# Graph layers on one core: neighbour rows by one-hot matmul for 60 buckets, by GpSimd row gathers for the other 38

## The chip, the cores and the metric

The kernel runs on one core of one Trainium2 chip. The metric is device microseconds of one execution. The kernel before was run 10 times; its median is the time that a change is measured against.

## The reference

A graph has N = 12500 nodes with 128 features and E = 200000 edges, sorted by `dst`. One gated layer is followed by three GIN layers; both parts end in a residual sum and a layernorm.

```python
# layer 0 (gnn)
msg      = (h[src] @ W_msg.T + b_msg) + edge_embed[edge_type]
messages = segment_sum(msg, dst)                  # rows of src are read, sums go to dst
x        = layernorm(x + gru_cell(messages, h))

# layers 1 to 3 (gin); every node also has an edge to itself
ee  = edge_attr @ enc_w + enc_b
h   = concat(x[dst], ee)          # layer 1: x[dst] + ee
agg = segment_sum(h, src)         # rows of dst are read, sums go to src
x   = relu(bn(agg @ w1 + b1)) @ w2 + b2
```

The last result is added to the layer's input `x` and normalised again.

## The kernel before

**Buckets and slots.** The nodes are cut into NB = 98 buckets of 128. Every pair (bucket summed into, bucket read from) is a cell with SL = 32 slots; a cell holds 20.8 edges on average. The few edges over 32 (some 190) go into an overflow list, which `spill(i)` adds by itself before each layer, 128 edges a round. The setup sorts the edges on chip under two keys (A and B), lists the overflow (`Listed`), and writes for each output bucket a row `inrow` (which row each slot reads) and columns `outcol` (which node each slot is summed into).

**One layer.** `layer(i, slot0)` goes over the output buckets o = 0 to 97. All feature rows of the graph, as three bfloat16 parts side by side (H3 = 384 columns, 768 bytes), lie in SBUF in 14 tiles `x0` to `x13` of 7 buckets each, loaded once a layer. For a bucket:

- `one_hots(o + 1)` loads the row `inrow` of the next bucket, broadcast to 128 partitions (`inr`, 784 KB, an SP transfer), and makes on DVE the gather matrix `g` in one compare (L1066) and the scatter matrix `s` in four (L1069).
- The 98 cells make 25 tiles of 128 slots, NTL = 25, in GROUPS = 9 groups of TG = 3 tiles. A group's gather is 12 matmuls (L1116) of 128 x 32, four of them beside each other in the array's column groups, from `x` into three PSUM banks `g` (two buffers). The result is evicted to `e` in bfloat16: in even groups two tiles on ACT (L1122) and one on DVE (L1123), in odd ones all three on ACT (L1125).
- One group later three scatter matmuls (L1087) multiply `e` by the scatter matrix and accumulate in the PSUM tile `acc` (one buffer). In layers 1 to 3 the bucket's own rows go into `acc` by one matmul with the identity (L1137); this is the edge of a node to itself.
- `finish(o)` adds the three parts in `acc` to the overflow sums (three adds on DVE, L1096 to L1098). After each odd bucket, the dense part of two buckets (`gru` in layer 0, `gin` after) is queued, and `tick()` emits a piece of it per group.

**Edge attributes.** The sums of `edge_attr` by `src` are the same for the three GIN layers and are made once by a generator, `attr`, in five steps per bucket. A step of `attributes()` issues 18 indirect DMAs on GpSimd back to back (L597; each brings 128 rows of 98 bytes), the others (`add_up`) make a one-hot on DVE, run 18 matmuls (L616), and store the result with an SP transfer. `gin` needs the sums of its buckets. The generator is stepped during the sort, and in layers 0 and 1 at these groups:

```python
                if slot0 is not None:
                    if k in (1, 5) or (k == 3 and o % 2):
                        next(attr, None)
```

That is 2.5 steps, half an attribute bucket, per output bucket.

**Order.** In the layers a scheduler orders each engine's instructions from the program and its tile dependencies. SP's queue carries `inr`, the overflow sums and the results; GpSimd's queue carries, within the layers, the attribute gathers alone, and between layers the spill's gathers (L501, L528, L554) and its write-back.

Of the kernel before, what the change touches and what calls it, by code (L numbers as in the profile page):

```python
# [18 lines left out]
H = 128  # L19
# [14 lines left out]

EP = 125
# [14 lines left out]
LCAP = E + 64  # L50
GL = 14
assert EP * EC == E and NB % GL == 0
# [3 lines left out]
def gnn_kernel(ctx: ExitStack, tc: tile.TileContext, x, xT, src, dst, ea, et, w_msg, w_ihT, w_hhT, b_msg,  # L56
# [256 lines left out]
    def xtiles(name):  # L313
        return [xpool.tile([P, XC, H3], BF16, name=f"x{k}") for k in range(NB // XC)]
# [4 lines left out]
    outcol = [cols.tile([P, NB, TC], BF16, name=f"outcol{i}") for i in range(2)]  # L319
# [4 lines left out]
    count = {k: ctile([1, 2], f"count{k}", I32) for k in "AB"}  # L324
# [9 lines left out]
    total = kp.tile([NB, 1], F32, name="total")  # L334
    startB = kp.tile([NB, 1], I32, name="startB")
# [140 lines left out]
    def starts():  # L476

        V.tensor_copy(cnt, cps[:NB, :NB])
        incl = kp.tile([NB, NB], F32, name="incl")
        V.tensor_tensor_scan(incl, ones[:NB, :NB], cnt, 0.0, op0=OP.mult, op1=OP.add)  # L480
        V.tensor_copy(total, incl[:, NB - 1:NB])
        rps = psa.tile([P, 512], F32, name="acc")
        T.matmul(rps[:NB, 0:1], before[:NB, :NB], total, start=True, stop=True)
        rst = kp.tile([NB, 1], F32, name="rst")
        V.tensor_scalar(rst, rps[:NB, 0:1], float(FRONT), None, op0=OP.add)
        V.tensor_copy(startB, rst)
        V.tensor_sub(incl, incl, cnt)
        V.tensor_scalar(start, incl, rst, None, op0=OP.add)


    def added(k, width, sources, target, pool_name):


        groups = nc.values_load(count[k][:, 1:2], min_val=0, max_val=LCAP // P,
                                skip_runtime_bounds_check_because="it counts groups of the edges")
        with tc.tile_pool(name=pool_name, bufs=1, side="right") as lp:
            with tc.For_i(0, groups, 1) as g:
                pos = lp.tile([P, 1], I32, name="pos")
                nc.sync.dma_start(pos, lists[k][bass.ds(g * P, P), :])
                key = lp.tile([P, 1], F32, name="key")  # L500
# [17 lines left out]
                node, rows = sources(top, field, lp)  # L518
# [27 lines left out]
    def spill(i):  # L546
        def sources(top, field, lp):
            s = lp.tile([P, 1], I32, name="s")
            V.tensor_add(s, top, field(11, 127))
            d = lp.tile([P, 1], I32, name="dd")  # L550
            V.scalar_tensor_tensor(d, field(18, 127), float(P), field(4, 127), op0=OP.mult, op1=OP.add)
            to, frm = (d, s) if i == 0 else (s, d)
            x3 = lp.tile([P, H3], BF16, name="x3")
            G.indirect_dma_start(out=x3, out_offset=None, in_=tables[i],  # L554
                                 in_offset=bass.IndirectOffsetOnAxis(ap=frm, axis=0))
            rows = lp.tile([P, H + NTX], F32, name="rows")
            V.tensor_tensor(rows[:, :H], x3[:, 0:H], x3[:, H:2 * H], op=OP.add)
            V.tensor_tensor(rows[:, :H], rows[:, :H], x3[:, 2 * H:], op=OP.add)
            if i:
                return to, rows[:, :H]  # L560
            t = lp.tile([P, 1], F32, name="t")
            V.tensor_copy(t, field(0, 15))
            V.tensor_scalar(rows[:, H:], iota[:, :NTX], t, None, op0=OP.is_equal)
            return to, rows

        added("A", H + NTX if i == 0 else H, sources, ovf[i], f"spill{i}")

    def spill_attributes():
        def sources(top, field, lp):
            s = lp.tile([P, 1], I32, name="s")  # L570
            V.tensor_add(s, top, field(18, 127))
            e3 = lp.tile([P, EW], BF16, name="e3")
            G.indirect_dma_start(out=e3, out_offset=None, in_=ea3,
                                 in_offset=bass.IndirectOffsetOnAxis(ap=field(0, (1 << 18) - 1), axis=0))
            rows = lp.tile([P, EA], F32, name="rows")
            V.tensor_copy(rows, e3[:, 0:EA])
            V.tensor_tensor(rows[:, 1:], rows[:, 1:], e3[:, EA:EA + DE], op=OP.add)
            V.tensor_tensor(rows[:, 1:], rows[:, 1:], e3[:, EA + DE:], op=OP.add)
            return s, rows

        added("B", EA, sources, ovfe, "spille")
# [100 lines left out]
    class Listed:  # L682
# [3 lines left out]
        def __init__(self, k, shift, bits):  # L686
            self.k, self.shift, self.bits = k, shift, bits
            self.stack = ExitStack()
            self.lp = self.stack.enter_context(tc.tile_pool(name=f"listed{k}", bufs=1, side="right"))
            t = lambda name, n, d=F32: self.lp.tile([P, n], d, name=name)  # L690
            self.back, self.same, self.at = t("back", SC), t("same", SC, I32), t("at", SC)
            self.first, self.base = t("first", 1), t("base", 1)
            self.m8, self.ok, self.row, self.spare, self.step = (t(n, 8) for n in ("m8", "ok", "row", "spare", "step"))
            self.rowi, self.val = t("rowi", 8, I32), t("val", 8, I32)
            self.num, self.most = t("num", 1), self.lp.tile([1, 2], F32, name="most")

        def mark(self, ahead):
# [18 lines left out]
            T.transpose(ps[0:1, 128:256], self.num, ident)  # L716
            G.iota(self.spare, pattern=[[P, 8]], base=LCAP, channel_multiplier=1,
# [11 lines left out]
            V.tensor_scalar(c[:, 1:2], self.most[:, 1:2], float(P - 1), None, op0=OP.add)  # L729
            V.tensor_single_scalar(c[:, 0:1], c[:, 0:1], 3, op=OP.logical_shift_right)  # L730
            V.tensor_single_scalar(c[:, 1:2], c[:, 1:2], 7, op=OP.logical_shift_right)
# [5 lines left out]
        def round(self):  # L737
# [7 lines left out]
            V.tensor_scalar(self.val, self.m8, self.base, None, op0=OP.add)  # L745
            for j in range(8):
# [5 lines left out]
        def rest(self):  # L752
            rounds = nc.values_load(count[self.k][:, 0:1], min_val=0, max_val=SC // 8,
                                    skip_runtime_bounds_check_because="it counts columns of the sort by eight")
            with tc.For_i(0, rounds, 1):
                self.round()

# [11 lines left out]
    def slots(cells):  # L769

        with tc.tile_pool(name="slots", bufs=1, side="right") as lp:
# [10 lines left out]
            def turned(rows, to):  # L782

                for t0 in range(0, NTL, 8):
                    n = min(8, NTL - t0)
# [32 lines left out]
            turned(sl, outcol[1])  # L818
# [5 lines left out]
            turned(ty, typecol)  # L824
            yield
# [32 lines left out]
    X = xtiles("0")  # L858
# [33 lines left out]
    with by_hand():  # L892
        la = Listed("A", SL, 18)
        for b in range(NB):
            runs(cells[:, b * SL:(b + 1) * SL], "A", start[:, b:b + 1], SL)
        for _ in la.mark(2):
            pass
# [155 lines left out]
    def layer(i, slot0):  # L1053
        a = 0 if i == 0 else 1
        wid = H3 + (NTX if i == 0 else 0)
        work = []

        def one_hots(o):

            inr = rp.tile([P, CW], BF16, name="inr")  # L1060
            nc.sync.dma_start(inr, inrow[a][o:o + 1, :].to_broadcast([P, CW]))
            g = ohp.tile([P, CW], BF16, name="g")
            st = ohp.tile([P, P, TC], BF16, name="s")
            ready.append((g, st))
            yield
            V.tensor_scalar(g, inr, pidx, None, op0=OP.is_equal)  # L1066
            yield
            for f0 in range(0, P, P // 4):
                V.tensor_tensor(st[:, f0:f0 + P // 4, :], iotas[:, f0:f0 + P // 4, :],  # L1069
                                outcol[a][:, o, None, :].to_broadcast([P, P // 4, TC]), op=OP.is_equal)  # L1070
                yield

# [4 lines left out]
        ready = []  # L1077
        for _ in one_hots(0):
            pass
        s = None  # L1080
        last = None

        def scatter(acc, st, e, k):
            for j in range(min(TG, NTL - TG * k)):
                t = TG * k + j
                m = P if t < NTL - 1 else P // 2
                T.matmul(acc[:, :wid], st[:m, :, t], e[:m, j, :wid], start=(i == 0 and t == 0),  # L1087
                         stop=(t == NTL - 1), skip_group_check=True)

        def finish(o, acc):  # L1090
            nonlocal s
            if o % 2 == 0:
# [6 lines left out]
            if i == 0:  # L1099
                V.tensor_add(so[:, H:], so[:, H:], acc[:, H3:wid])  # L1100
            if o % 2:
                work.append((gru if i == 0 else gin)(i, o - 1, s))

        for o in range(NB):
            g, st = ready.pop(0)
            pieces = one_hots(o + 1) if o + 1 < NB else iter(())
            acc = None
            for k in range(GROUPS):
                n = min(TG, NTL - TG * k)
# [11 lines left out]
                if n == TG and k % 2 == 0:  # L1121
# [4 lines left out]
                if i == 0:  # L1126
# [3 lines left out]
                if last:  # L1130
                    scatter(*last)
                    if k == 0:
                        finish(o - 1, last[0])
                if k == 0:
                    acc = psa.tile([P, 512], F32, name="acc")
                    if i:
                        T.matmul(acc[:, :H3], identb, piece(X, o), start=True, stop=False, skip_group_check=True)  # L1137
                last = (acc, st, e, k)
                tick()
                next(pieces, None)  # L1140
                if slot0 is not None:
                    if k in (1, 5) or (k == 3 and o % 2):
                        next(attr, None)
            for _ in pieces:
                pass
        scatter(*last)
        finish(NB - 1, last[0])
# [3 lines left out]
    for i in range(4):  # L1151
        if i:
            X = xtiles(str(i))
            for k in range(NB // XC):
# [3 lines left out]
        layer(i, (0, NB, None, None)[i])  # L1158
# [41 lines left out]
```

## Time and profile before

| what | us |
|---|---|
| median of 10 runs | 8898.17 |
| lowest and highest run | 8883.45 and 8905.03 |
| the profiled execution | 8896.35 |
| its span, first to last instruction | 8894.5 |
| layer 0, first compare of g to that of layer 1 | about 2448 |
| layer 1 | about 2020 |
| layer 2 | about 1319 |
| layer 3 | about 1350 |

Busy time over the span: PE 5923.2 us (67%), DVE 4282.4 (48%), ACT 3672.5 (41%), GpSimd (POOL) 1978.8 (22%); the mean granted clock of TensorE is 0.808. All times below come from that one execution unless a median is named. In the profile, PE is the matmul engine and PEld its weight loads, which overlap the matmuls; "L1116" is line 1116 of the kernel. A group line gives the line, engine and operation, the tiles written and read, the count, then busy time, mean nanoseconds of one, and the idle time before them with what ended it. "remote" there is a releaser on another engine which the profile could not name.

### The profile page before, as it was taken

The numbers are of one execution on the slowest core, as the hardware profiler recorded it, in microseconds if no ns is written. First come the engines' busy times: TensorE is split into PE (matmuls) and PEld (weight loads), VectorE is DVE, ScalarE is ACT, GpSimd is POOL, SyncE is SP. The second block draws the span as 40 slices with busy tenths as digits, with TensorE's granted clock in tenths as the row PEclk, the third lists the DMA queues.
The fourth block names the chain that finished last, engine by engine and source line by source line (L and its number), as shares of the span: only waits on it lengthen the run. The fifth ranks groups of instructions, "written<-read, shape, count | busy, mean of one in ns | idle before, by whom it ended". The sixth has DMA issues, their size and how long they took to land. (4 is left out here: it accounts for less than half of the span.)

```text
span 8894.5 us, 137018 instructions
## 1 busy us (share of the span) xinstructions
PE 5923.2 (67%) x56001; PEld 3117.5 (35%) x56001; DVE 4282.4 (48%) x9941; ACT 3672.5 (41%) x4747; POOL 1978.8 (22%) x1963
## 2 busy tenths in 40 slices
PE   0765130166566566666466666699799999799998
PEld 0464020023222222222233333344344444444444
DVE  8398774444344344443333333355444554455554
ACT  0300020033333333333233333366566666566666
POOL 0000667433333333333233333300000000000000
PEclk9655565577777777777677777799899999899999
DMA  7300131212122121222211111122322222222221
GB/s 167 121 8 10 20 80 23 38 49 58 43 56 57 43 57 47 53 58 65 71 48 51 46 47 51 50 75 78 109 78 77 77 78 92 92 83 79 80 82 66
DMA packets 482010, 569.25 MB, mean 64 GB/s; under 512 B 116846, under 2 KB 422554, under 8 KB 480512
## 3 DMA queue, kind: packets, MB, share of 16 engines
q1 hardware_dynamic: 377338, 512.73, 17.9%
q0 software_dynamic: 61376, 26.26, 3.0%
q10 hardware_dynamic: 42664, 21.50, 0.9%
q8 instruction: 438, 7.18, 0.3%
q14 instruction: 194, 1.59, 0.1%
HBM read 452.05 MB, written 108.23 MB: 63 GB/s over the span
## 5 line engine op out<-in xcount | busy, mean ns | idle before, releaser
L1087 PE MATMUL acc<-e,s 128*128 128x384 bf16 (+3 forms) x9800 | 2416.4, 357 | 1135.2 <-ACT e L1125 489.7
L1116 PE MATMUL g<-x,g 128*32 128x384 bf16 x38416 | 2525.2, 347 | 356.1 <-DVE e L1123 256.4
L1125 ACT CAST e<-g 128x1152 bf16<-128x1152 f32 (+1 forms) x1960 | 1909.5, 990 | 1496.4 <-PE g L1116 766.7
L597 POOL DMA_INDIRECT eat<-ea,eidcol x1764 | 1805.3, 1023 | 2774.0 <-PE d L616 2186.8
L1087 PEld LDWEIGHTS <-s 128*128 128x128 bf16 (+1 forms) x9800 | 1290.3, 151 | 2060.2 <-issue 1912.7
L1123 DVE CAST e<-g 128x384 bf16<-128x384 f32 x1568 | 868.5, 554 | 2177.7 <-ACT e L1122 2122.5
L1122 ACT CAST e<-g 128x768 bf16<-128x768 f32 x1568 | 1256.7, 801 | 1404.0 <-PE g L1116 935.5
L1116 PEld LDWEIGHTS <-g 128*32 128x32 bf16 x38416 | 860.4, 97 | 1671.6 <-issue 1424.5
L1069 DVE TENSOR_TENSOR s<-iotas,outcol 128x832 bf16<-128x832 bf16 x1568 | 894.5, 584 | 0.0
L1066 DVE TENSOR_SCALAR g<-inr,pidx 128x3136 bf16<-128x3136 bf16 x392 | 406.0, 1036 | 297.7 <-PE g L1116 277.3
L1128 DVE TENSOR_TENSOR e<-iota,typecol 128x30 bf16<-128x30 f32 (+1 forms) x882 | 159.6, 182 | 586.8 <-remote 486.6
L501 POOL DMA_INDIRECT key<-sortedA,pos x8 | 7.7, 956 | 1887.8 <-DMA pos<-listA 1887.8
L626 ACT COPY ownT<-d 102x128 bf16<-102x128 bf16 x98 | 26.1, 266 | 713.0 <-PE d L624 406.5
L1096 DVE TENSOR_TENSOR s<-s,acc 128x128 f32<-128x128 f32 x392 | 113.0, 288 | 375.0 <-PE acc L1087 364.9
L473 PE MATMUL acc<-ob,oa 125*98 125x98 bf16 x1600 | 271.1, 343 | 14.5 <-DVE ob L471 14.4
L1029 ACT ACTIVATE gates<-d,shift,scale 128x256 f32<-128x256 f32 x294 | 150.1, 561 | 312.3 <-PE d L1027 312.3
L473 PEld LDWEIGHTS <-oa 125*98 125x98 bf16 x1600 | 270.9, 259 | 22.6 <-DVE oa L468 12.1
L416 PE MATMUL split<-at,ident 125*125 125x512 f32 x100 | 79.9, 926 | 209.9 <-DMA at<-in_ea 139.9
L616 PE MATMUL d<-eat,eoh 128*128 128x49 bf16 x1764 | 144.9, 225 | 110.4 <-DVE eoh L611 99.5
L418 ACT CAST st<-split 125x512 bf16<-125x512 f32 x150 | 85.8, 611 | 318.4 <-PE split L416 190.6
L270 DVE TENSOR_TENSOR keyA<-keyA 128x1024 f32<-128x1024 f32 x153 | 187.0, 1222 | 48.2 <-ACT keyA L287 35.6
L624 PE MATMUL d<-identb,own 128*102 128x128 bf16 x98 | 26.7, 273 | 255.9 <-DVE own L588 254.9
(297 smaller groups left out, 4667.0 us busy)
## 6 DMA issues: line engine op xcount, KB each, us to landing
inr<-inrow SPq DMA_DIRECT2D x392, 784.0 KB
eat<-ea,eidcol POOLq DMA_INDIRECT x1764
table<-x SPq DMA_DIRECT2D x147, 192.0 KB
ovf<-z SPq DMA_DIRECT2D x3, 6400.0 KB
ea<-st SPq DMA_DIRECT2D x25, 765.6 KB
s<-ovf SPq DMA_DIRECT2D x147, 128.0 KB
x<-table ACTq DMA_DIRECT2D x21, 672.0 KB
x<-table SPq DMA_DIRECT2D x21, 672.0 KB
```

The lines of the kernel that those rows point to most:

```text
L270: V.tensor_tensor(l2, lo, hi, op=OP.min)
L473: T.matmul(cps[:NB, :NB], oa[:, :, c], ob[:, :, c], start=(c0 + c == 0), stop=(c0 + c == EC - 1))
L597: G.indirect_dma_start(out=at[:, t, :], out_offset=None, in_=ea3, in_offset=bass.IndirectOffsetOnAxis(ap=eidcol[:, b, t:t + 1], axis=0))
L1029: A.activation(h1[:, m, :], ph[:, m, :], AF.Relu, bias=w["shift"][:, i - 1, m:m + 1], scale=w["scale"][:, i - 1, m:m + 1])
L1066: V.tensor_scalar(g, inr, pidx, None, op0=OP.is_equal)
L1069: V.tensor_tensor(st[:, f0:f0 + P // 4, :], iotas[:, f0:f0 + P // 4, :], outcol[a][:, o, None, :].to_broadcast([P, P // 4, TC]), op=OP.is_ ...
L1087: T.matmul(acc[:, :wid], st[:m, :, t], e[:m, j, :wid], start=(i == 0 and t == 0), stop=(t == NTL - 1), skip_group_check=True)
L1116: T.matmul(pg[c * SL:(c + 1) * SL, j, :H3], g[:, b * SL:(b + 1) * SL], piece(X, b), start=True, stop=True)
L1122: A.copy(e[:, :2, :H3], pg[:, :2, :H3])
L1123: V.tensor_copy(e[:, 2, :H3], pg[:, 2, :H3])
L1125: A.copy(e[:m, :n, :H3], pg[:m, :n, :H3])
L1128: V.tensor_tensor(e[:m, :n, H3:], iota[:m, None, :NTX].to_broadcast([m, n, NTX]), typecol[:m, o, t:t + n, None].to_broadcast([m, n, NTX]), ...
```

## The change

In layers 1 to 3 only the edges whose `dst` lies in the first IC = 60 buckets keep slots: 15 tiles in five groups, of 60 gather and 15 scatter matmuls a bucket. The other edges of an output bucket, up to 896 of them, form RT = 7 more tiles of 128 edges. Their rows are fetched from the table in DRAM by seven indirect DMAs on GpSimd (`fetch`, 128 rows of 768 bytes each), three output buckets ahead, into four tiles that take turns in the place of `x9` to `x12`, and are summed by seven matmuls straight from there (`scatter_rows`). Only nine tiles of `x` are loaded. The own row of buckets from 63 on is loaded by an SP transfer (`own_row`). Evictions in these layers are all on ACT. The scatter of a bucket's last group, the last of its seven row tiles and `finish` stand in group 0 of the next bucket; the accumulator of the new one is first used in group 1. Edges beyond 896 of a bucket have an overflow list of their own, and spill reads a third counter for it.

The setup gains `row_windows`, which makes the row numbers (`rowcol`) and output columns of the 896 edges with one indirect DMA, DVE fields and PE transposes, beside the listing of the overflow; 15 tiles of `outcol[1]` are turned there instead of 25.

The generator `attr` is stepped 3.5 times a bucket in layer 0 and once a bucket in layer 1. In order, the changed kernel issues 307 of the attribute gathers before layer 0, 1239 in it and 218 in layer 1. Each of layers 1 to 3 issues 686 row fetches.

```diff
+IC = 60
+CT = IC // 4
+RT = 7
+WA = RT * P
+TW = CT + RT
+FAR = 1 << 19
-LCAP = E + 64
+LCAP = 2 * E + 128 - 2 * E % 128 + P
...
-    def layer(i, slot0):
-        a = 0 if i == 0 else 1
-        wid = H3 + (NTX if i == 0 else 0)
+    def layer(i, pace):
+        cells_only = i == 0
+        a, nb, tiles, tw = (0, NB, NTL, TC) if cells_only else (1, IC, CT, TW)
+        wid = H3 + (NTX if cells_only else 0)
+        groups = -(-tiles // TG)
...
-            nc.sync.dma_start(inr, inrow[a][o:o + 1, :].to_broadcast([P, CW]))
+            nc.sync.dma_start(inr[:, :nb * SL], inrow[a][o:o + 1, :nb * SL].to_broadcast([P, nb * SL]))
...
+        def fetch(o):
+            if cells_only or o >= NB:
+                return
+            t = xpool.tile([P, RT, H3], BF16, name=f"x{XF + o % RB}")
+            for j in range(RT):
+                G.indirect_dma_start(out=t[:, j, :], out_offset=None, in_=tables[i],
+                                     in_offset=bass.IndirectOffsetOnAxis(ap=rowcol[:, o, j:j + 1], axis=0))
+            fetched[o] = t
+
+        def own_row(o):
+            if o < XF * XC:
+                return piece(X, o)
+            t = own_rows[:, o % XC, :]
+            nc.sync.dma_start(t, tables[i][o * P:(o + 1) * P, :])
+            return t
...
+        for o in range(RB - 1):
+            fetch(o)
...
+        def scatter_rows(o, st, j0, j1):
+            for j in range(j0, j1):
+                T.matmul(sums[o][:, :H3], st[:, :, CT + j], fetched[o][:, j, :], start=False, stop=False,
+                         skip_group_check=True)
...
-                if n == TG and k % 2 == 0:
+                if cells_only and n == TG and k % 2 == 0:
                     A.copy(e[:, :2, :H3], pg[:, :2, :H3])
                     V.tensor_copy(e[:, 2, :H3], pg[:, 2, :H3])
                 else:
                     A.copy(e[:m, :n, :H3], pg[:m, :n, :H3])
...
-                if last:
+                if k == 0:
+                    if last:
+                        if not cells_only:
+                            scatter_rows(o - 1, last[1], RT - 1, RT)
+                        scatter(*last)
+                        finish(o - 1)
+                else:
+                    if k == 1:
+                        sums[o] = psa.tile([P, 512], F32, name="acc")
+                        if not cells_only:
+                            T.matmul(sums[o][:, :H3], identb, own, start=True, stop=False, skip_group_check=True)
                     scatter(*last)
+                    if not cells_only and k > 1:
+                        scatter_rows(o, st, 2 * k - 4, 2 * k - 2)
+                if k == 0 and not cells_only:
+                    own = own_row(o)
+                    fetch(o + RB - 1)
...
-                if slot0 is not None:
-                    if k in (1, 5) or (k == 3 and o % 2):
-                        next(attr, None)
+                if pace(o, k):
+                    next(attr, None)
...
-            X = xtiles(str(i))
-            for k in range(NB // XC):
+            X = xtiles(XF)
+            for k in range(XF):
...
-        layer(i, (0, NB, None, None)[i])
+        layer(i, (lambda o, k: k in (1, 3, 5) or k == 7 and o % 2, lambda o, k: k == 3)[i] if i < 2
+              else lambda o, k: False)
```

## The prediction

> **What bounds the kernel now.** I read the page's forty slices first, then the stretches of one stage beside each other, then the timeline of one line as a clock, and last the waits.
>
> ```profile
> PE   0765130166566566666466666699799999799998
> ACT  0300020033333333333233333366566666566666
> POOL 0000667433333333333233333300000000000000
> PEclk9655565577777777777677777799899999899999
> ```
>
> A slice is 222 us. GpSimd (POOL) works only up to slice 26; there PE stands at 5 to 6 tenths at a granted clock of 7 tenths. In the last 14 slices (layers 2 and 3) GpSimd is silent, and PE is at 9 tenths at nearly full clock. So layers 2 and 3 are bound by PE, and something that comes with GpSimd costs the earlier layers time. The one-hot compare L1066 starts once a bucket and serves as the clock. Its columns are start, duration, engine, line, operation, tiles, shapes, count, and in brackets the idle time before it with its releaser:
>
> ```profile
> 5211.87 1.04 DVE L1066 TENSOR_SCALAR g<-inr,pidx 128x3136 bf16<-128x3136 bf16 x1 [0.53 <-PE g L1116]
> 5243.37 1.04 DVE L1066 TENSOR_SCALAR g<-inr,pidx 128x3136 bf16<-128x3136 bf16 x1 [1.06 <-PE g L1116]
> 5259.01 1.04 DVE L1066 TENSOR_SCALAR g<-inr,pidx 128x3136 bf16<-128x3136 bf16 x1 [0.53 <-PE g L1116]
> ...
> 6895.88 1.04 DVE L1066 TENSOR_SCALAR g<-inr,pidx 128x3136 bf16<-128x3136 bf16 x1 [0.36 <-PE g L1116]
> 6907.72 1.03 DVE L1066 TENSOR_SCALAR g<-inr,pidx 128x3136 bf16<-128x3136 bf16 x1 [0.70 <-PE g L1116]
> 6921.81 1.04 DVE L1066 TENSOR_SCALAR g<-inr,pidx 128x3136 bf16<-128x3136 bf16 x1 [0.36 <-PE g L1116]
> ```
>
> Layer 2 takes 11.84 and 14.09 us for two buckets, 25.9 a pair, 12.95 each. Layer 1 takes 31.50 us for a bucket in which GpSimd issues its 18 attribute gathers (L597) and 15.64 for the next, 47.1 a pair. A burst of 18 costs 21.2 us per pair; against a bare bucket the bursting one alone loses 31.5 − 12.95 = 18.5 us, 1.03 us a gather. Stretches of that burst beside a quiet pair (columns: window, length, busy time and count on PE, PE's weight loads, DVE, ACT and POOL, granted clock, DMA share, GB/s):
>
> ```profile
> 5215.30:5219.30 4.00, 3.76 (x42) 1.91 (x45) 3.64 (x13) 1.52 (x2) 3.08 (x4) 1.00 0.23 66
> 5219.30:5227.30 8.00, 4.32 (x43) 1.79 (x36) 1.57 (x5) 2.19 (x3) 6.17 (x7) 0.76 0.14 17
> 5227.30:5240.80 13.50, 2.20 (x15) 0.75 (x15) 0.00 (x0) 1.12 (x1) 8.05 (x9) 0.50 0.10 9
> 6900.00:6925.90 25.90, 24.01 (x265) 12.70 (x264) 12.97 (x29) 17.40 (x23) 0.00 (x0) 1.00 0.24 82
> ```
>
> The quiet pair runs 265 matmuls in 25.9 us, 10.2 per us. The burst runs 42 in its first 4 us (no loss), 43 in the next 8, 15 in the last 13.5. After the first stretch no engine is busy, and the DMA share falls. The inside of the burst shows why:
>
> ```profile
> 5225.80 1.15 PE L1116 MATMUL g<-x,g 128*32 128x384 bf16 x12
> ...
> 5233.10 0.94 POOL L597 DMA_INDIRECT eat<-ea,eidcol  x1 [0.30 <-issue]
> 5233.76 1.12 ACT L1125 CAST e<-g 128x1152 bf16<-128x1152 f32 x1 [8.20 <-remote]
> ...
> 5234.93 1.12 PE L1087 MATMUL acc<-e,s 128*128 128x384 bf16 x3 [7.97 <-ACT e L1125]
> ```
>
> The twelve gather matmuls begin at 5225.80 and are done some 1.2 us later; the eviction that reads them starts only at 5233.76, 8.20 us idle, and the scatter behind it waits for the eviction. PE's signal to ACT arrives late while GpSimd issues indirect DMAs, until some 4 us after the last one starts. What delays it the trace does not say.
>
> **What is taken off PE, layers 1 to 3.** A quiet step of layer 2:
>
> ```profile
> 7501.29 0.67 PE L1116 MATMUL g<-x,g 128*32 128x384 bf16 x12
> 7501.94 0.66 PE L1087 MATMUL acc<-e,s 128*128 128x384 bf16 x3
> 7502.53 0.67 PE L1116 MATMUL g<-x,g 128*32 128x384 bf16 x12
> ```
>
> One group takes 1.24 us from gather to gather: 0.60 for 12 narrow matmuls (four side by side), 0.05 each, and 0.64 for 3 scatter matmuls, 0.213 each. Per bucket the change removes 38 gather matmuls (−1.90) and 10 scatter matmuls (−2.13) and adds 7 matmuls over fetched rows, of the scatter's shape (+1.49): −2.54 us. At each bucket's start PE waits for DVE's share of the eviction, in layer 2 and 3 57.5 us over 77 buckets, 0.75 each; that share goes to ACT, and the accumulator is first used one group later: −0.75. Together −3.3, a quiet bucket of 9.65 us. ACT then has 5 evictions of 1.12, 5.6 us a bucket, under PE's; the smaller compares leave DVE further behind. Both cost nothing.
>
> **What is added on GpSimd.** Seven indirect DMAs a bucket. The spill's fetch of 768-byte rows takes 0.95 us to issue like the 98-byte attribute gather, and a burst repeats every 1.25 us:
>
> ```profile
> L597 POOL DMA_INDIRECT eat<-ea,eidcol x1764 | 1805.3, 1023 | 2774.0 <-PE d L616 2186.8 <-issue 497.1 <-DMA outrow<-dl 46.2
> L554 POOL DMA_INDIRECT x<-table,dd x6 | 5.7, 946 | 17.0 <-DVE s L549 17.0
> ```
>
> 7 × 1.25 = 8.75 us a bucket, under 9.65, so GpSimd does not bound by itself, and rows come three buckets early. Each fetch waits for the rows of the bucket before to be summed; behind it on GpSimd stand the next fetches and, in layer 1, attribute gathers, which have buckets of slack. The own row of buckets 63 on becomes an SP transfer before the accumulation, a group ahead; the loads of inr shrink from 784 to 480 KB, so SP gains.
>
> The cost that decides is x, what seven fetches do to PE's signals in a bucket. No burst of row fetches stands in this trace, so x is bounded. Below nothing: excluded, since GpSimd's work speeds nothing up. Lower end 0: the delay might belong to the attribute work alone. From the attribute burst: seven starts end at 7.5 us, signals are free 4.25 us after (as there), so 11.75 us are touched; the first 4 are free, and the rest at 43 instead of 82 matmuls per 8 us loses 3.7 us. Over all 31 bursts from 4300 to 5600 us the trace has 70 matmuls in the first 12 us, against 122 quiet: 5.1 us. Upper end: 7 × 1.03 = 7.2, with the refilling of the pipeline. I take 5.5, near the mean of all bursts with a little refilling, as the issue rows are the same for both kinds of row. That is 294 × (5.5 − 3.3) = +647 us.
>
> The Trainium skill, "SBUF — State Buffer", section "Who interferes with whom", says that DMA never contends with a compute engine. By it x would be 0 and the change worth −970. The burst's rows, 100 matmuls in 25.5 us where 260 fit, disagree. The page "TensorE: Matmul & The Clock Gate", part on the clock gate, halves the clock after an idle window of about 3.4 us; by it a short burst with shorter gaps would cost no clock, and x would lean to the lower end.
>
> **The rest.** Attribute buckets move forward: layer 0 steps the generator 3.5 times a bucket instead of 2.5 (69 attribute buckets for 49), layer 1 once (12 for 35), three more run in the sort. At 21.2 us each in either layer, +424 and −488, and the three in the sort cost 0 to 63: −30. Each of layers 1 to 3 begins with 21 fetches: 26 us and 4 of late signals, in which at the burst's rate (100 of 260) a third of the work goes on: +20 each, +60. Nine x tiles instead of 14 load beside the spill loop; 0. Sorting row indices needs one indirect DMA and some transposes beside the listing of overflow edges: 0 to 10, and 15 instead of 25 tiles of outcol turned gives that back: 0. Counted from the inputs, the far edges of a bucket are 892 at most, below 896, so no new overflow loop runs.
>
> Sum: 647 − 30 + 60 = +677. On the profiled execution, 8896.35 us (span 8894.5 and 1.85 around it), that is 9573; the median of the runs, 8898.17, stands 2 us higher, so 9575. The ten runs lie within 8883 to 8905, so some 0.2% (18 us) can be told from no change.
>
> **Rivals.** (1) Slower by the forecast's mechanism: x from 3.4 to 7.2, its body from 3.9 to 7, which gives 9100 to 10010; chance 0.53. (2) Full price: every fetch delays PE by 1.03 to 1.18 us (21.2 / 18), x 7.2 to 8.2, 294 × 3.9 to 4.9 + 30: 10075 to 10370; for it speaks that the late signals last past the last DMA, against it the free first 4 us. Chance 0.17. (3) The other side, faster: the row fetches leave PE's signals alone, because the delay hangs on the small rows or on what the attribute step does on PE and DVE around them. Place: the eviction's wait for PE in layers 2 and 3. From x below 3.2 it decides; at x = 0, −970 + 30, 7960; a delay that is only half of the burst's, x = 2.5, gives 8690. For it: DMA share is low and 768 bytes suit a transfer better; against: in the burst it is signals, not data, that are late. Chance 0.29 for all below 8880, of which 0.14 near 7960. (4) The change does not act as said, or all cancels within 0.2%: x between 3.1 and 3.3, chance 0.01.
>
> **How the numbers follow.** Slower 0.53 + 0.17, with 0.01 same and 0.29 faster. Forecast 9575; the likeliest case's own range is 9100 to 10010. Eight in ten need the full price's lower part and more than half of the faster cases: 8150 to 10150 leaves out 0.12 below and some 0.07 above.
>
> **What would show it.** Right: in layers 2 and 3 the slices of PE at 5 to 7 tenths, the clock below 0.9, POOL at 6 tenths, evictions that start several us after the matmuls they read, buckets of about 15 us. Wrong: buckets of 10 us with PE at 9 tenths (x near 0), or, above 16.5 us, fetches that wait for one another. Layer 0 should grow by about 420 us and layer 1 shrink by 488 less 98 times the bucket's change; if the moved attribute steps cost otherwise, that sum is wrong, not x.

## The result, and the profile after

The changed kernel takes 9039.85 us (median of 8 runs, 9001.78 to 9065.35), before 8895.65 us (28 runs): ratio 1.0164, 95% interval 1.0152 to 1.0176. It is slower, by 144 us and not by 677. The time lies in the wide range (8150 to 10150) and just below that of the likeliest case (9100 to 10010); the size of the change was wrong by more than a factor of four.

In the profiled execution the span went from 8894.5 to 9030.2 us, +136. From the first compare of `g` in a layer to that of the next:

| us | layer 0 | layer 1 | layer 2 | layer 3 |
|---|---|---|---|---|
| before | 2448 | 2020 | 1319 | 1350 |
| after | 2744 | 1721 | 1386 | 1430 |
| difference | +296 | −299 | +67 | +79 |

The forecast was +424, −252, +236 and +236. The forty slices of the page after, 226 us each:

```profile
PE   0764130256655555656636556775777776677776
POOL 0001567344443444444445556443555543545543
PEclk6655565577777777777767778887888888889988
```

In the last 12 slices, layers 2 and 3, GpSimd is at 3 to 5 tenths, and PE stands at 6 to 7 tenths where it stood at 9 before. The inside of a bucket of layer 2 (start, duration, engine, line, operation, tiles, idle time before with its releaser):

```profile
7006.12 0.36 PE L1264 MATMUL g<-x,g 128*32 128x384 bf16 x4 [0.36 <-issue]
...
7007.86 0.72 DVE L1183 TENSOR_SCALAR g<-inr,pidx 128x1920 bf16<-128x1920 bf16 x1 [5.10 <-PE g L1264]
...
7009.65 1.11 PE L1228 MATMUL acc<-e,s 128*128 128x384 bf16 x3 [3.17 <-ACT e L1273]
...
7014.02 1.00 POOL L1196 DMA_INDIRECT x<-table,rowcol  x1 [7.88 <-PE acc L1233]
```

Four gather matmuls start at 7006.12 and take 0.36 us. The compare, which by the profile waits for them, starts at 7007.86, and the scatter, which waits for an eviction, at 7009.65 after 3.17 us idle. That is the forecast mechanism, in smaller portions than in the attribute burst. The wait lines of 6500 to 7500 us (engine, tile, line waited for: us in total, times, longest):

```profile
POOL x L1196 <- PE acc L1233: 337.7, 68, 8.7
DVE g L1183 <- remote: 331.8, 52, 7.2
...
ACT e L1273 <- remote: 141.8, 80, 4.0
PE acc L1228 <- ACT e L1273: 139.6, 59, 3.7
```

Measured over 656 PE instructions of that stretch, from the modelled end to the next event of their semaphore: median 0.21 us, a quarter over 1.54 us, the longest 4.9 us. The next event can be an earlier instruction's that came late, so the true delays are rather longer. In 244 of the 308 that are over 0.5 us, PE had started and finished a later instruction before the event: it is the signal that is late, not PE. Signals of ACT and DVE take 0.01 us in the median; their tails can't be read, since the trace has only 369 events for 484 ACT instructions and 542 for 667 of DVE. So the pairs of buckets in layers 2 and 3 take 27.25 and 26.92 us (medians) where before took 25.9: +0.6 us a bucket, not +2.2.

### The profile page after: what moved, and what is told of

Its sections match the earlier page's. It is cut to its first block, busy times and chain, and to the rows that moved or that the text cites. A ratio compares the mean times of both kernels' runs of the same rounds, so it can differ in the third digit from the quotient of the medians.

```text
span 9030.2 us, 112084 instructions
## 1 busy us (share of the span) xinstructions
PE 5263.2 (58%) x43956; PEld 2953.4 (33%) x43956; DVE 3542.4 (39%) x8831; ACT 2956.0 (33%) x3575; POOL 4023.5 (45%) x4022
## 3 DMA queue, kind: packets, MB, share of 16 engines
q0 software_dynamic: 160240, 229.05, 11.3%
## 5 line engine op out<-in xcount | busy, mean ns | idle before, releaser
L1228 PE MATMUL acc<-e,s 128*128 128x384 bf16 (+2 forms) x6860 | 1764.1, 377 | 1968.5 <-ACT e L1273 1025.1
L1196 POOL DMA_INDIRECT x<-table,rowcol x2058 | 2009.2, 976 | 1884.7 <-PE acc L1233 1250.1
L1264 PE MATMUL g<-x,g 128*32 128x384 bf16 x27244 | 1845.7, 366 | 237.5 <-issue 124.8
L1228 PEld LDWEIGHTS <-s 128*128 128x128 bf16 (+1 forms) x6860 | 963.7, 151 | 2588.9 <-issue 2329.5
L1183 DVE TENSOR_SCALAR g<-inr,pidx 128x1920 bf16<-128x1920 bf16 (+1 forms) x392 | 314.0, 801 | 2075.6 <-remote 1337.6
L1186 DVE TENSOR_TENSOR s<-iotas,outcol 128x704 bf16<-128x704 bf16 (+1 forms) x1568 | 816.2, 534 | 0.0
L1233 PE MATMUL acc<-x,s 128*128 128x384 bf16 x2058 | 631.1, 379 | 28.1 <-DMA x<-table,rowcol 25.9
L1270 ACT CAST e<-g 128x768 bf16<-128x768 f32 x392 | 313.3, 799 | 847.5 <-remote 500.7
L1271 DVE CAST e<-g 128x384 bf16<-128x384 f32 x392 | 217.7, 555 | 630.2 <-ACT e L1270 530.9
L1233 PEld LDWEIGHTS <-s 128*128 128x128 bf16 x2058 | 303.9, 148 | 235.7 <-issue 206.2
```

Source lines behind the costliest of these rows:

```text
L1183: V.tensor_scalar(g[:, :nb * SL], inr[:, :nb * SL], pidx, None, op0=OP.is_equal)
L1196: G.indirect_dma_start(out=t[:, j, :], out_offset=None, in_=tables[i], in_offset=bass.IndirectOffsetOnAxis(ap=rowcol[:, o, j:j + 1], axis=0))
L1228: T.matmul(sums[o][:, :wid], st[:m, :, t], e[:m, j, :wid], start=(cells_only and t == 0), stop=(t == tiles - 1), skip_group_check=True)
L1233: T.matmul(sums[o][:, :H3], st[:, :, CT + j], fetched[o][:, j, :], start=False, stop=False, skip_group_check=True)
L1264: T.matmul(pg[c * SL:(c + 1) * SL, j, :H3], g[:, b * SL:(b + 1) * SL], piece(X, b), start=True, stop=True)
L1270: A.copy(e[:, :2, :H3], pg[:, :2, :H3])
```

## The experiments

One fact stands before all of them. The experiments ran on chips 0, 3, 11, 12 and 15 (11 twice), and there the kernel before takes 7270 us and not 8896. Each run is therefore compared with before and with the changed kernel on such chips. The expectations of the first four runs were written for a before of 8896 us.

**The kernel before, where its signals are on time.** No edit.

> The kernel before, for its trace where signals of PE are on time. Quiet buckets 12.95 us as in the profile before (PE binds them), buckets with an attribute burst near 14 us instead of 31: layer 1 at some 1330 us instead of 2020, layer 0 near 1450 instead of 2448; total 7270. Where PE's signals are late, 8898 and the stages of the profile before.

7267.47 us. Stages 1443, 1394, 1319 and 1348 us, layer 1 being 64 us over what was expected; quiet pairs 25.92 us, exactly as on record. Layers 2 and 3, without GpSimd, are the same to 3 us; the two with GpSimd are 1005 and 626 us shorter. A stretch of layer 1 (window, length, busy time and count on PE, PEld, DVE, ACT, POOL, granted clock, DMA share, GB/s):

```profile
3300.00:4300.00 1000.00, 945.31 (x10301) 510.02 (x10302) 551.62 (x1334) 647.41 (x837) 554.95 (x558) 0.99 0.31 83
```

558 gathers of GpSimd stand beside 10.3 matmuls per us at a clock of 0.99. In the record's burst, 92 matmuls shared 25.5 us with 18 gathers. (The prediction's 100 adds three stretches, and each counts again the matmuls that cross its border; the view of the whole stretch has 92.) The same instruction stream thus has the late signals on the record's chip and not on these.

**The changed kernel there.** No edit; twice.

> The changed kernel as it is, beside the kernel before. Before took 8898 us in the profiled run of the prediction and 7270 us beside the runs without fetches, where signals of PE were on time while GpSimd issued its gathers. Theory H (the late signals belong to the chip that a run lands on, and the rest of the working holds): where before takes about 7270 us, the changed kernel loses nothing to a burst and takes about 6570 us, ratio 0.90; where before takes about 8898 us, ratio 1.016 as on record. Rival K (the lateness comes and goes by itself, whatever the chip): a ratio between these, and times that scatter by more than 1%.

> The changed kernel beside the kernel before. Theory H: where before takes 7270 us, 6582 us; where it takes 8896 us, 9040 us.

6582.11 us, ratio 0.9051 (0.9036 to 0.9066), and 6575.03 us, ratio 0.9045 (0.9019 to 0.9071). Theory H holds in its first half: where signals are on time the change is a gain of 9.5%. Its other half rests on the record alone. PE's signals take 28 ns in the median, 30 ns for nine in ten, over 760 instructions of layer 2. Stages 1620, 1240, 968, 999 us.

**No fetches.**

```diff
+            if o >= RB:
+                fetched[o] = rowtiles[o % RB]
+                return
```

> The changed kernel, but in layers 1 to 3 only the first four buckets' rows are fetched; later buckets sum those rows again, so the row sums are wrong and all matmuls, evictions and one-hots stay. Layers 2 and 3 of the changed kernel take 13.6 us a bucket (27.2 a pair). Theory 1 (the price x of a burst of seven was smaller than I took, the saving of 3.3 us on PE was right): buckets of 9.65 us, x = 13.6 - 9.65 = 3.95, time about 9040 - 294 x 3.95 - 60 = 7820 us. Rival 2 (x is 5.5 as forecast and the saving on PE was larger, 4.85 us): buckets of 8.1 us, about 7360 us.

> The changed kernel without row fetches after the first four buckets of a layer, row sums wrong by that. Where PE's signals are on time, 6240 us again. Where they are late: buckets of layers 2 and 3 still 8.85 us, the attribute bursts at their price, 294 x 4.75 + 45 = 1440 us less than the changed kernel, 7600 us; a rival in which the quiet bucket is dearer there, 9.65 us, gives 7840 us.

6240.21 us, ratio 0.8577 (0.8563 to 0.8592), and 6242.12 us. The absolute times expected for the first run were meant for late signals and can't be read. The bucket can: pairs of 17.69 us, 8.85 a bucket, against 12.95 before. Neither 9.65 nor 8.10: the saving on PE is 4.1 us, between the two theories. A step of it, and the wait of the gathers over 4500 to 5200 us:

```profile
4801.80 0.67 PE L1268 MATMUL g<-x,g 128*32 128x384 bf16 x12
4802.40 0.72 PE L1232 MATMUL acc<-e,s 128*128 128x384 bf16 x3
4802.96 0.49 PE L1237 MATMUL acc<-x,s 128*128 128x384 bf16 x2
4803.37 0.67 PE L1268 MATMUL g<-x,g 128*32 128x384 bf16 x12
```

```profile
L1268 PE MATMUL g<-x,g 128*32 128x384 bf16 x4748 | 257.4, 329 | 0.0
L1232 PE MATMUL acc<-e,s 128*128 128x384 bf16 x1185 | 253.4, 334 | 0.0
```

A group with two row matmuls takes 1.57 us where a group took 1.24: 0.165 us for a row matmul, not 0.213. These gathers and scatters wait for nothing; before, over 6400 to 7400 us, they waited 57.5 + 15.6 us in 77 buckets, 0.95 each:

```profile
L1116 PE MATMUL g<-x,g 128*32 128x384 bf16 x7570 | 454.9, 330 | 57.5 <-DVE e L1123 57.5
L1087 PE MATMUL acc<-e,s 128*128 128x384 bf16 (+1 forms) x1934 | 435.8, 336 | 15.6 <-ACT e L1125 13.3
```

**Order and evictions alone**, on the kernel before:

```diff
-                if n == TG and k % 2 == 0:
+                if i == 0 and n == TG and k % 2 == 0:
...
+                    if k == 1:
+                        accs[0] = psa.tile([P, 512], F32, name="acc")
```

> The kernel before (all 98 buckets by slots, no fetch) with two parts of the change alone, in layers 1 to 3: all evictions on ACT, and the new bucket's accumulator first used in group 1. Without fetches the changed kernel's quiet bucket was 8.85 us, 4.1 less than before's 12.95 and not 3.3 less as I summed. Theory S (2.54 by the counts of matmuls stands, and order and evictions are worth 1.56, not 0.75): quiet buckets of 11.4 us, 294 x 1.56 = 459 us less than before. Rival C (order and evictions are worth the 0.75 that the wait rows show, and the matmuls taken away were dearer): 12.2 us, 220 us less.

7189.97 us, ratio 0.989 (0.9873 to 0.9906), 82 us less; pairs of 25.42, so 0.25 us a bucket. Both theories are wrong: with nine groups the evictions, all on ACT, are waited for again:

```profile
L1125 ACT CAST e<-g 128x1152 bf16<-128x1152 f32 x558 | 562.6, 1049 | 111.9 <-PE g L1116 100.3 <-PE acc L1088 1.0
L1116 PE MATMUL g<-x,g 128*32 128x384 bf16 x6074 | 354.7, 330 | 24.6 <-ACT e L1125 21.7 <-DMA x<-table 3.0
```

Over the 62 buckets of that window, PE waits 24.6 us before gathers and 21.0 before scatters, 0.74 us a bucket. In the run without fetches, with five groups and row matmuls between them, they are gone; no run tells which of the two does it.

**The same bytes by SP.**

```diff
-                G.indirect_dma_start(out=t[:, j, :], out_offset=None, in_=tables[i],
-                                     in_offset=bass.IndirectOffsetOnAxis(ap=rowcol[:, o, j:j + 1], axis=0))
+                b = (o + 14 * j) % NB
+                nc.sync.dma_start(t[:, j, :], tables[i][b * P:(b + 1) * P, :])
```

> The changed kernel, with each of the seven row fetches of a bucket replaced by a plain SP transfer of 128 rows from the table, the same bytes into the same tiles at the same place; the rows are those of one bucket, not of the edges. Theory G (PE's signals are late because GpSimd issues DMAs): as without fetches, some 7820 us, up to 100 more for SP's queue. Rival T (the transfers themselves, their bytes or their landing, hold PE up): near the changed kernel, 9040 us, within 100.

> The same bytes by SP transfers instead of GpSimd fetches, rows of one bucket instead of the edges' rows. Where PE's signals are on time, 6225 us again. Where they are late: theory G (GpSimd's issue delays them) 7600 us, rival T (the transfers do) 9040 us.

6225.01 us and 6227.34 us, ratios 0.856 and 0.8567: as without fetches, 17.69 a pair. Transfers of these bytes cost nothing there. What the changed kernel pays over 6240 us it then pays for GpSimd's issuing or for the scattered rows, which this run does not have; the runs with five and with fourteen fetches below tell these apart. On a chip with late signals this wasn't seen, so theory G is not decided for the record.

**Fetches spread over the groups.**

```diff
+                fetch_rows(o + RB - 1, (0, 2, 4, 5, 6)[k] if k < 5 else RT, (2, 4, 5, 6, 7)[k] if k < 5 else RT)
```

> The changed kernel with the same seven fetches a bucket issued two, two, one, one, one over the five groups instead of seven in the first. Theory B (a burst is free for its first 4 us and is dear after): short bursts are nearly free, buckets near 11 us, some 8300 us. Rival D (every fetch delays PE's signals by its own share, 0.55 us each, wherever it stands): no change beyond 0.5%, 9040 us.

> The fetches issued two, two, one, one, one over the five groups, beside the changed kernel on the same chip. Theory B (a burst is free for its first 4 us): where signals are late, buckets near 11 us and 294 x 2.5 = 700 us less than the changed kernel. Rival D (each fetch delays by its own share): within 1% of the changed kernel. Where signals are on time, both theories say within 1% of the changed kernel.

6571.6 us (0.9039) and, beside the changed kernel on one chip, 6577.35 us (0.9047 against 0.9051): no difference. Whether it helps where signals are late stays open.

**Five fetches of seven, and fourteen.**

```diff
-            for j in range(RT):
+            for j in range(RT if o < RB else 5):        # or: [*range(RT), *range(RT)]
```

> The changed kernel with five of a bucket's seven row fetches issued in layers 1 to 3; the other two row tiles keep the rows of the first four buckets, so those sums are wrong. Where PE's signals are on time, the changed kernel's layers 2 and 3 take 40 us each more than without fetches. Theory I (GpSimd's issue time, 7 x 1.3 = 9.1 us a bucket, is just over PE's 8.85): five fetches are hidden, layers 2 and 3 at 928 and 959 us, layer 1 shorter by 196 x 1.3 = 255 or down to its 979, in all 6250 to 6330. Rival M (each fetch holds PE up a little, 0.06 us): layers 2 and 3 give back 2/7 of 40, 11 us each, in all 6300 to 6550. Where signals are late: a bucket is 2/7 of 4.75 = 1.4 us shorter, 400 us less than the changed kernel.

> The changed kernel with every row fetch of layers 1 to 3 issued twice into the same tile, 14 a bucket; the result is the same. Where PE's signals are on time, theory I: GpSimd's issue binds, 14 x 1.3 = 18.2 us a bucket, layers 2 and 3 at 1800 us each, layer 1 at 2100, in all 9100. Rival M (0.06 us a fetch): 41 us more a layer, some 6700. Where signals are late: 4.75 us more a bucket at least, 10400.

Five: 6361.64 us, ratio 0.8747 (0.8732 to 0.8761), layers 2 and 3 at 932 and 964 us, pairs of 17.69 as with none. Fourteen: 9323.18 us, ratio 1.2819 (1.2793 to 1.2844), pairs near 37.8. That is theory I: where signals are on time, GpSimd's issue is a second bound beside PE's 8.85 us, nothing below it and all above it. Only layer 1 gave back less than expected for five, 147 us of 255, and so the total came out 32 us above its range. GpSimd binds only part of that layer: the attribute gathers end at bucket 62, and between buckets 10 and 60 a bucket takes 13.7 us with seven fetches and 11.3 with five, where from 70 to 90 it takes 9.1 and 8.9. GpSimd's groups, and PE's row matmuls beside them, in the changed kernel at 4700 to 5500 us, then GpSimd's with fourteen fetches at 6700 to 8000:

```profile
L1196 POOL DMA_INDIRECT x<-table,rowcol x608 | 615.2, 1012 | 185.2 <-issue 174.9 <-DMA x<-table,rowcol 6.4 <-PE g L1264 4.0
L1233 PE MATMUL acc<-x,s 128*128 128x384 bf16 x608 | 164.3, 331 | 26.2 <-DMA x<-table,rowcol 25.8
```

```profile
L1198 POOL DMA_INDIRECT x<-table,rowcol x929 | 904.8, 974 | 335.8 <-issue 237.2 <-DMA x<-table,rowcol 59.5 <-PE acc L1235 12.2
```

Busy and idle time of the first make 1.32 us a fetch; seven are 9.2 us, just over 8.85. GpSimd is hardly idle for anything but issue, and PE waits for fetched rows, 0.3 us a bucket: GpSimd is the bound of layers 2 and 3, by 0.4 us a bucket.

**The new pace alone, on the kernel before, and the old pace on the changed kernel.**

```diff
-                    if k in (1, 5) or (k == 3 and o % 2):
+                    if (k in (1, 3, 5) or k == 7 and o % 2) if i == 0 else k == 3:
```

```diff
-        layer(i, (lambda o, k: k in (1, 3, 5) or k == 7 and o % 2, lambda o, k: k == 3)[i] if i < 2
+        layer(i, (lambda o, k: k in (1, 5) or k == 3 and o % 2, lambda o, k: k in (1, 3) or k == 2 and o % 2)[i] if i < 2
```

> The kernel before with only the new pace of the attribute generator: 3.5 steps a bucket in layer 0, one in layer 1. Theory E (an attribute bucket costs the same 21 us in either layer): layer 0 about +420, layer 1 about -490, in all 8870 us, within 40. Rival L (it costs less in layer 0 where it is dense, 14.8 us as layer 0 of the changed kernel grew by 296 for 20 of them): layer 1 -490, layer 0 +296, in all about 8700 us.

> The changed kernel with the old pace of the attribute generator, 2.5 steps a bucket in layers 0 and 1 (half an attribute bucket). Where signals are on time, theory P (GpSimd's issue time binds where both kinds of gather meet: 1.29 us a gather): layer 1 has 686 + 630 gathers, 1700 us instead of 1240, layer 0 some 165 less; in all 6580 + 295 = 6875 us. Rival N (attribute gathers hide anywhere): layer 1 as it is, layer 0 165 less, 6415 us. Where signals are late: layer 0 296 less, layer 1 23 bursts of 15 to 21 us more, 9040 + 50 to 190.

The pace alone: 7435.35 us, ratio 1.0226 (1.0209 to 1.0244). Layer 0 takes 1615 us for 1443, layer 1 1381 for 1394: where attribute gathers hide, moving them only makes GpSimd the bound of layer 0 (1239 gathers of 1.3 us are 1611 us). The prices expected were for late signals. The old pace on the changed kernel: 6853.51 us, ratio 0.9427 (0.9411 to 0.9442); layer 0 1445 us, layer 1 1687 us for 1240. Theory P said 6875 and 1700: the 686 fetches and the attribute gathers share one engine, and layer 1 lasts as long as it issues.

**A version between the two**: layer 1 by slots for all buckets with the order and evictions of the experiment above, the old pace in both layers, and the fetches in layers 2 and 3 only. Two lines of its edit; the others lay out the columns and row numbers for it.

```diff
-        cells_only = i == 0
+        cells_only = i < 2
...
-        layer(i, (lambda o, k: k in (1, 3, 5) or k == 7 and o % 2, lambda o, k: k == 3)[i] if i < 2
+        layer(i, (lambda o, k: k in (1, 5) or k == 3 and o % 2) if i < 2
```

> A version between the two: layer 1 by slots for all 98 buckets, with evictions on ACT and the accumulator in group 1, and the old pace of the attribute generator in layers 0 and 1; layers 2 and 3 as in the changed kernel. Where PE's signals are on time, theory P (in layers 0 and 1 of the changed kernel GpSimd's issue binds): layer 0 1445, layer 1 1366, layers 2 and 3 968 and 999, in all some 6530 us, 50 less than the changed kernel and 0.898 of before. Rival N (the changed kernel's layer 1 is bound otherwise and 12.95 us a bucket come back in it): 6700 us or more. Where signals are late: layers 0 and 1 as before, layers 2 and 3 some 145 us more than before, 9040 us.

6554.89 us, ratio 0.901 (0.8995 to 0.9025), against 0.9051 (0.9036 to 0.9066) for the changed kernel: stages 1449, 1374, 966 and 1007 us. It beats the kernel before by 9.9%. Against the changed kernel the difference is 0.4% between two chips, and the changed kernel's second ratio, 0.9045 (0.9019 to 0.9071), overlaps: no gain over it is shown. On the record's chip it wasn't run.

## Why the prediction was right or wrong

**Right: the direction on record, the mechanism as far as the trace shows it, the order of the layers.** The direction holds on that machine alone; elsewhere the same change gains 9.5%. On record, PE's signals are late while GpSimd issues row fetches too, layer 0 grew and layer 1 shrank, and layers 2 and 3, which gained nothing from the pace, ended slower. "Rows come three buckets early" held: between 6500 and 7500 us on record PE waited for no fetched row, over all of layer 2 four times, 10.2 us together. Of the signs that were named, the slices of PE and the clock (0.88 over 6500 to 7500 us) came; GpSimd at 6 tenths and buckets of 15 us did not.

**Wrong, first term: the saving on PE, 3.3 us forecast and 4.1 measured.** I priced matmuls one by one, as a share of their group. Four groups go: three full ones of 1.24, 3.72 us, which is what I had for them, and the short ninth of two gathers and one scatter, some 0.58 us, where I had 0.31. It stands in the run with the order alone (0.27 from the first of these lines to the second, 0.31 from the third to the fourth):

```profile
5306.59 0.34 PE L1116 MATMUL g<-x,g 128*32 128x384 bf16 x2
5306.86 0.15 PEld L1088 LDWEIGHTS <-s 128*128 128x128 bf16 x1 [0.17 <-issue]
...
5308.40 0.38 PE L1088 MATMUL acc<-e,s 64*128 64x384 bf16 x1
5308.71 0.67 PE L1116 MATMUL g<-x,g 128*32 128x384 bf16 x12
```

That is 4.30 and not 1.90 + 2.13 = 4.03. Seven row matmuls cost 7 × 0.165 = 1.16 and not 1.49: six scatter matmuls behind each other take 0.98 us in the run without fetches, 0.16 each (from 4809.03 to 4810.01 us), so the 0.64 for three held some 0.15 us that is paid once a group, and I charged it for each row matmul again. The gathers' and scatters' waits go, 0.95 and not 0.75. Together 4.30 − 1.16 + 0.95 = 4.1. Over 294 buckets the step is worth 0.8 × 294 = 235 us. The wait was not worth its 0.75 by itself: with nine groups the order and the evictions bring 0.25.

**Wrong, second term: x, 5.5 us forecast and about 4.7 on record.** Layers 2 and 3 of the changed kernel take 13.63 and 13.46 us a bucket on record (medians), and 8.85 without fetches elsewhere; before's quiet bucket is 12.95 us in both places, which is why I take the difference, 4.6 to 4.8. No run without fetches came to a chip with late signals, so it is a difference and not a measurement by itself. It lies in the bounds that I gave, 3.7 to 7.2. Both readings below my 5.5 were miscounted. The view of 5215.3 to 5227.3 us has 77 matmuls, and not 42 + 43; and from 4300 to 5600 us the trace has 28 bursts and not 31, with 77 matmuls in their first 12 us, in the mean and in the median, and not 70. Against 122 that is 4.4 us either way, and with the little refilling that I added it would have been near the 4.7; that a burst of seven costs what the first 12 us of an attribute burst cost is not shown by that. (Nor is it so that "no engine is busy" in the burst: GpSimd is, for 6.17 of 8 us.) This is another 0.8 × 294 = 235 us.

**The rest.** Layer 0 grew by 296 us for 20 attribute buckets, 14.8 each, where I took 21.2 from layer 1; the whole of layers 0 and 1 came to −3 us against +172. The first four buckets of layers 2 and 3 took 28 and 29 us more than before, of which some 2 are the buckets' own: 26 and 27, where I took 20. The setup took 7 us less (the first compare is at 1749.5 for 1756.7), where I took 0. Two terms that I subtracted from each other, each off by 0.8 us and both to the side of slower, made 2.2 us a bucket out of 0.6.

**What I did not see: that the same kernel can run without the cost.** The forecast read the late signals as what GpSimd's DMAs do to PE. On five chips they do nothing of the kind. There rival 3 came true, with x = 0.4 us, and for another reason than I gave it: not small rows against large ones, since attribute bursts are free there as well. Its estimate at x = 0 was a gain of 940 us; it measured 690, since I had left out that GpSimd's issue time binds where attribute gathers and row fetches meet: "under 9.65, so GpSimd does not bound by itself" fails against 8.85 us, with 1.32 us a fetch and not 1.25, by 40 us in each of layers 2 and 3 (968 and 999 against 928 and 959); and layers 0 and 1 are 177 and 261 us longer by it (1620 against 1443 at the old pace; 1240 against 979 without fetches). The rule of the Trainium skill, "SBUF — State Buffer", section "Who interferes with whom", that DMA never contends with a compute engine, agrees with the runs on those chips (seven SP transfers a bucket leave pairs at 17.69 us). On record PE's signals were late beside GpSimd's DMAs, 0.21 us in the median, but no run shows that the DMAs contend with PE, so the record does not settle the rule.

**What stays open.** Why PE's signals are late on the record's machine, and whether it is the chip, its state or what else ran there: both traces of the record show it, and by their times all 28 and 8 runs there have it, none of the six groups of runs after. Late signals come together: the 308 that were over 0.5 us late between 6500 and 7500 us share 155 events. Of these events 50 came within 0.15 us of the end of an indirect DMA, where an even spread would put 24. That is a coincidence in time, not a cause shown. The record's trace also lacks events of ACT and DVE where GpSimd works and has all of them in layers 2 and 3 of before; whether the recording itself has a part in this was not tested.

## What to carry to other kernels

Price a change that removes whole groups by the group, from start to start, and what it adds by what stands beside it: a short group cost more than its share of matmuls (0.58 us for 0.31), a matmul added to a group less (0.165 for 0.213). Read the count of a stretch in one window; stretches side by side count twice what crosses their borders. When a profile shows an engine late for no reason that it names, find out first whether the machine or the kernel does that: the sign of a change can hang on it, here +1.6% against −9.5%. And add up an engine's issue time for all that shares it in a stage; in layers 2 and 3 GpSimd cost nothing at five fetches a bucket, and was the bound at seven.

## What the runs showed of the hardware

On the record's machine the kernel before takes 22% longer and the changed one 37% longer than on the other chips, with the same instructions, the same quiet buckets (25.92 us a pair in both) and nearly the same durations on GpSimd (976 ns a row fetch on record, 1004 in the changed kernel elsewhere). An indirect DMA of 128 rows of 768 bytes costs GpSimd 1.25 us from start to start in an undisturbed burst, and 1.32 to 1.34 on average over the stretches read. Seven plain SP transfers of 128 rows a bucket beside PE cost nothing that 17.69 us a pair would show.
